# Another order and another queue for the first eight microseconds of a two-layer kernel

## The chip, the cores and the metric

The kernel runs on one core of a Trainium2 chip. The metric is the device time of one execution in microseconds (us). Before the change it is 358.14 us, the median of three runs (357.95 to 358.57).

The core's engines are named as the profile names them: PE is TensorE (matmul), PEld its loads of weights (the stationary operand, 128 columns), DVE is VectorE, ACT is ScalarE, POOL is GpSimd and SP is SyncE. SP and ACT both issue DMAs; each has a queue of its own. In a profile line, `f_0gu<-xt,w` means that tile f_0gu is written from xt and w.

## The reference

The input x has the shape 4 x 512 x 256 (batch, positions, features). There are two layers of the form

```
xn = layernorm(x)
s  = mixer(xn)                    # layer 0: a linear recurrence of one step; layer 1: causal attention
h  = silu(xn @ W1.T) * (xn @ W3.T)    # 256 -> 1024
g  = silu(fwht(h) @ W2.T)             # fwht: Walsh-Hadamard transform along the 1024
x  = x + s * g
```

The change touches only the start of layer 0: the layernorm of batch 0, its transposition, and the first products with W1 and W3.

## The kernel before, in words

**Numbers.** A matrix that goes into a product is split into a high part (a cast to fp32r by ACT) and a low part (the difference, by DVE); `split` (L59) does both. A product is then three matmuls: high x high, low x high, high x low. So each operand has two producers, one after the other: ACT's cast and DVE's subtraction.

**Work.** Batches are worked off one after the other. `ffn` (L474) makes the hidden layer in eight chunks `c` of 128 features. For each chunk there are two PSUM tiles `gu` (the gate from W1 and the linear part from W3), filled by the up products. ACT applies silu to the first, DVE multiplies by the second. The up weights w13 come in four quarters of 512 columns, each for two chunks; a quarter is one DMA from HBM, ACT's cast and DVE's subtraction. `load_w13` (L114) issues the DMA; the first quarter is fetched in two halves of 256 columns, one for each of chunks 0 and 1. `split_w13` (L122) makes the parts; for the first quarter each half by itself.

**The first batch.** `load_x` (L99) fetches x in four pieces of 128 positions, by SP's queue and ACT's in turn. `norm_first` (L381) is a generator. Up to its first yield it writes the layernorm's statistics and the normalised tiles `xn`, two pairs of tiles, on DVE, with the power -0.5 on POOL. After it come the transposes on PE, whose other operand is the identity (fetched at L949), in two groups of four (one per pair of tiles), then ACT's casts into the high part of `xt` (L426) and DVE's subtractions into the low part (L429). The first pair goes into two PSUM tiles, one per half of the features, so that it takes two casts; the second goes into one and takes one. For chunk 0 the up products are done separately for the first and the second pair (`parts=2`, L518), in the order w high x x high, w low x x high, w high x x low (L526), each with two halves of the features and two PSUM tiles: twelve matmuls of 256 columns per pair.

**Fillers.** `zero_products` (L944) multiplies a tile of zeros `zr` by itself into a PSUM tile `warm` that nobody reads. `norm_first` puts eleven of them ahead of the first group of transposes and two between the groups. Each is a matmul of 512 columns.

**What sets the order.** The program is written through a layer that records instructions and schedules them; `after(ins)` (L471) holds an instruction behind another one on its engine. The order of each queue is then fixed. The main code (L934 to L971) issues in this order: the four pieces of x (SP and ACT in turn), ACT's load of the silu table with a tiny activation (L937), the memset of `zr` (L941), on SP the identity, the halves of the first quarter, the second quarter, the two halves of w2 (`load_w2`), the Hadamard matrix, quarters 2 and 3, and the mixer's weights. `prep_first` (L974) prepares w2 beside the products. SP issues its DMAs one after the other; from the ninth DMA of the program on, an issue also waits until an earlier DMA that uses the same semaphore has landed.

On ACT, as built, the order after the table is: the cast of w13's first half, the three casts of x, the cast of the second half, the cast of quarter 1, silu of chunk 0, the cast of quarter 2, silu of chunk 1, the cast of the Hadamard matrix. On DVE: the memset, statistics and normalising, low part of w13's first half, three low parts of x, low part of the second half, two operations of w2's preparation, the gate product of chunk 0, two more of w2, low part of quarter 1.

Of the kernel before, what the change touches and what calls it, by code (L numbers as in the profile page):

```python
# [21 lines left out]
P = 128  # L22
D = 256
B = 4
S = 512
# [10 lines left out]
def kernel(ctx: ExitStack, tc: tile.TileContext, a: dict, out: bass.AP):  # L36
# [16 lines left out]
    def small(name):  # L53
        return act.tile([P, NT], F32, tag="small", name=name, bufs=16)
# [4 lines left out]
    def split(src, hi, lo, engine=nc.vector):  # L59

        h = nc.scalar.copy(hi, src)  # L61
        return h, engine.tensor_tensor(lo, src, hi.bitcast(F32), ALU.subtract)  # L62
# [51 lines left out]
    def load_w13(layer, q):  # L114

        raw = t4(f"w13raw_{layer}_{q}", [P, 2, S])
        n = 2 if (layer, q) == (0, 0) else 1
        for cs in (slice(i * S // n, (i + 1) * S // n) for i in range(n)):
            nc.sync.dma_start(raw[:, :, cs], a[f"w13_{layer}"][q][:, :, cs])
        return raw  # L120

    def split_w13(layer, q, raw):  # L122
        both = wp.tile([P, 2, 2, S], F32R, tag="w13", name=f"w13_{layer}_{q}", bufs=4)
        hi, lo = both[:, 0], both[:, 1]
        if q:

            with after(first["silus"][q - 2] if q > 1 else None):
                split(raw, hi, lo)
            return hi, lo
        halves = [slice(c * D, (c + 1) * D) for c in range(2)]  # L130
        split(*(z[:, :, halves[0]] for z in (raw, hi, lo)))
        next(normed)
        with after(first["norm"][0]), after(first["norm"][1]):
            hi_, lo_ = split(*(z[:, :, halves[1]] for z in (raw, hi, lo)))
        first["w13"] = hi_, lo_
        return hi, lo

    def load_w2(layer):
# [242 lines left out]
    def norm_first():  # L381

        xn = act.tile([P, NT, D], F32, tag="xn", name="xn0_0", bufs=3)
        hi, lo = xTs[0, 0] = xt_pair("xt0_0")
        xns[0, 0] = xn
        x = xs[0]
        ins, pairs = None, []
        for i in range(2):
            st = act.tile([P, NT, 6], F32, tag="stats", name=f"ln0_0st{i}", bufs=4)
            mv = act.tile([P, NT, 2], F32, tag="mv", name=f"ln0_0mv{i}", bufs=4)  # L390
            r = small(f"ln0_0r{i}")
            with after(ins):
                for t in (2 * i, 2 * i + 1):
                    ins = nc.vector.bn_stats(st[:, t, :], x[:, t, :])
                for t in (2 * i, 2 * i + 1):
                    with after(ins):
                        nc.vector.bn_aggr(mv[:, t, :], st[:, t, :])
                rs = r[:, 2 * i : 2 * i + 2]
                ins = nc.vector.tensor_scalar(
                    rs, mv[:, 2 * i : 2 * i + 2, 1], LN_EPS, None, ALU.add  # L400
                )
            nc.gpsimd.tensor_tensor(rs, rs, mhalf[:, :2], ALU.pow)
            pairs.append((mv, r))
        for i, (mv, r) in enumerate(pairs):
            for t in (2 * i, 2 * i + 1):
                with after(ins):
                    ins = nc.vector.tensor_scalar(
                        xn[:, t, :], x[:, t, :], mv[:, t, 0:1], r[:, t : t + 1], ALU.subtract, ALU.mult
                    )
        yield  # L410

        hi_ = lo_ = None
        ins = zero_products(11)
        for i in range(2):
            ts_ = slice(2 * i * P, 2 * (i + 1) * P)

            ks = (slice(0, 2),) if i else (slice(0, 1), slice(1, 2))
            os = [psum(f"xt0_0tp{i}{j}", [P, k.stop - k.start, 2 * P]) for j, k in enumerate(ks)]
            with after(ins):
                for t in (2 * i, 2 * i + 1):  # L420
                    for o, k in zip(os, ks):
                        for n in range(k.start, k.stop):
                            ins = transpose(o[:, n - k.start, sl(t - 2 * i)], xn[:, t, sl(n)], ident)
            for o, k in zip(os, ks):
                with after(hi_):
                    hi_ = nc.scalar.copy(hi[:, k, ts_], o)  # L426
            for o, k in zip(os, ks):
                with after(lo_):
                    lo_ = nc.vector.tensor_tensor(  # L429
                        lo[:, k, ts_], o, hi[:, k, ts_].bitcast(F32), ALU.subtract  # L430
                    )
            if i == 0:
                with after(ins):
                    ins = zero_products(2)
        first["norm"] = hi_, lo_
        yield

# [33 lines left out]
    def after(ins):  # L471
        return tc.issue_after(ins.ins) if ins else nullcontext()

    def ffn(name, xT, w13, w2, slot, defer=1, spare=(), parts=1, behind=False, tail=()):  # L474

# [31 lines left out]
        for c in range(NH):  # L509
            with after(gates[-2] if behind and c >= 2 else None):  # L510
                wh, wl = w13(c // 2)
            gu = []
            for j in range(2):

                o = psum(f"{name}gu{c}_{j}", [P, S], **(DN[0] if behind and c == 1 else GU))
                cols = slice((c % 2) * D + j * P, (c % 2) * D + (j + 1) * P)
                gu.append((o, cols))
            for half in range(parts if c == 0 else 1):  # L518
                n = S // (parts if c == 0 else 1)
                ts_ = slice(half * n, (half + 1) * n)  # L520
                if parts == 1 or c:
                    for o, cols in gu:
                        last_up = mm3(o[:, ts_], k_pairs((wh, wl), cols, xT, ts_))
                    continue

                for n, (w, x) in enumerate(((wh, xT[0]), (wl, xT[0]), (wh, xT[1]))):  # L526
                    for k in range(2):
                        for o, cols in gu:
                            last_up = matmul(
                                o[:, ts_], w[:, k, cols], x[:, k, ts_],  # L530
                                start=n + k == 0, stop=n + k == 3,
                            )
            gu = [o for o, _ in gu]
            h = hid(f"{name}h{c}")
            first["silu"] = nc.scalar.activation(h, gu[0], AF.Silu)
            first.setdefault("silus", []).append(first["silu"])
            gates.append(nc.vector.tensor_tensor(h, h, gu[1], ALU.mult))  # L537
            first["gate"] = gates[-1]
            if c < len(spare):
                hh, hl = spare[c]  # L540
            else:
                hh = hid(f"{name}hh{c}", F32R)
                hl = hid(f"{name}hl{c}", F32R)
            if c < len(spare):
                nc.scalar.copy(hh, h)
                late.append((hl, h, hh))
            else:
                split(h, hh, hl)
            for _ in range(2 if c >= NH - 2 else 0):
                if late:  # L550
                    lo_, h_, hi_ = late.pop(0)
                    with after(gates[-1]):
                        nc.vector.tensor_tensor(lo_, h_, hi_.bitcast(F32), ALU.subtract)
            queue.append((c, hh, hl))
            ups = last_up if behind else None
            with after(gates[-1] if behind else None), after(ups):
                slot(2 * c)
            if len(queue) > defer:
                down(*queue.pop(0))
            with after(gates[-1] if behind else None), after(ups):  # L560
                slot(2 * c + 1)
# [371 lines left out]

    load_x(0, 1, (nc.sync, nc.scalar))  # L934

    table = small("table")
    nc.scalar.activation(table, mhalf, AF.Silu)  # L937


    zr = hid("zr", F32R)  # L940
    nc.vector.memset(zr.bitcast(F32), 0.0)  # L941
    warm = psum("warm", [P, S], tag="dn", bufs=2)

    def zero_products(n):  # L944
        for _ in range(n):
            ins = matmul(warm, zr[:, :P], zr, start=True, stop=True)
        return ins

    nc.sync.dma_start(ident, a["ident"])  # L949
    raw13 = [load_w13(0, q) for q in range(2)]  # L950
    raw2 = load_w2(0)
    nc.sync.dma_start(had_f, a["hadamard"])
    raw13 += [load_w13(0, q) for q in range(2, 4)]
# [56 lines left out]
        yield  # L1010


    dn = None
    for b in range(B):
        tasks = []
        if b == 0:
            prep = prep_first()
            next(prep)
            tasks.append((prep, 12))
        if b:  # L1020
            tasks.append((call(gate_all, f"g0_{b - 1}", dn, xns[0, b - 1], xs[b - 1]), 1))
# [26 lines left out]
            tasks.append((prep_s(3), 4))  # L1048
        bg = Beside(*tasks)
        if b == 0:  # L1050
            dn = ffn("f0_0", xTs[0, 0], w13, w2, bg.slot, NH, spare, parts=2, behind=True)
        else:
            tail = [run(atts[0].tq, j) for j in range(2)] if b + 1 == B else []
            dn = ffn(f"f0_{b}", xTs[0, b], w13, w2, bg.slot, tail=tail)
# [152 lines left out]
```

## Time and profile before

| | |
|---|---|
| three runs, us | 357.95, 358.14, 358.57 |
| span of the profiled execution | 356.7 us (its own time is not listed; the median lies 1.5 above the span) |
| busy: PE, PEld, DVE, ACT, POOL | 350.9, 327.5, 287.2, 197.8, 20.8 us |
| mean granted clock of TensorE | 0.998 |
| eleven zero products | from 1.45 to 6.31 us, four transposes follow |
| first up product | starts at 7.84 us |
| issues: x by ACT and by SP | 0.73 and 1.18 us each |
| issues: identity, w13's halves, quarter 1 | 1.65, 2.11, 2.81, 3.45 us, all by SP |
| landed: x (four pieces), identity | 3.23, 3.43, 3.84, 4.06; 5.66 us |
| landed: w13's halves, quarter 1, w2's first half | 6.85, 7.56, 9.67, 10.97 us |

The page gives each engine's busy time and the chain of work that ended last, followed back from the last instruction. The timeline gives instructions in order of time, neighbours of the same kind merged, and in brackets how long the engine was idle before and who ended it. Matmuls overlap in the records, since PE takes the next one up before the last has drained: what counts between two matmuls is the distance of their starts. A landing is the last of a DMA's sixteen increments of its semaphore, one for each DMA engine. All times are from the span's start.

### The profile page before, as it was taken

The numbers are of one execution on the slowest core, as the hardware profiler recorded it, in microseconds if no ns is written. First come the engines' busy times: TensorE is split into PE (matmuls) and PEld (weight loads), VectorE is DVE, ScalarE is ACT, GpSimd is POOL, SyncE is SP. The second block draws the span as 40 slices with busy tenths as digits, with TensorE's granted clock in tenths as the row PEclk, the third lists the DMA queues.
The fourth block names the chain that finished last, engine by engine and source line by source line (L and its number), as shares of the span: only waits on it lengthen the run. The fifth ranks groups of instructions, "written<-read, shape, count | busy, mean of one in ns | idle before, by whom it ended". The sixth has DMA issues, their size and how long they took to land.

```text
span 356.7 us, 6276 instructions
## 1 busy us (share of the span) xinstructions
PE 350.9 (98%) x2477; PEld 327.5 (92%) x2477; DVE 287.2 (81%) x598; ACT 197.8 (55%) x374; POOL 20.8 (6%) x22
## 2 busy tenths in 40 slices
PE   8999999999999999999999999999999999999995
PEld 6878998888988898888999999999999999999994
DVE  6899659998579938998887957989679897678646
ACT  3666166265463425674467655586555676556443
POOL 2000110300020210100110001100011000000000
PEclk9999999999999999999999999999999999999999
DMA  6935000301044317656257145662554635445401
GB/s 208 367 98 205 2 1 2 117 0 61 0 167 163 145 38 230 257 174 191 118 208 265 36 172 209 217 201 115 206 187 168 230 158 206 143 152 186 199 2 59
DMA packets 16284, 52.25 MB, mean 146 GB/s; under 512 B 1632, under 2 KB 7936, under 8 KB 16256
## 3 DMA queue, kind: packets, MB, share of 16 engines
q1 hardware_dynamic: 15968, 51.60, 40.8%
q8 instruction: 19, 0.31, 0.4%
q10 hardware_dynamic: 288, 0.26, 0.2%
q14 instruction: 9, 0.07, 0.1%
HBM read 42.40 MB, written 9.45 MB: 145 GB/s over the span
## 4 chain that ended last, share of the span: by engine, by line
PE 98%; DVE 1%; ACT 0%; issue 0%
PE f_0dn L70 6%; PE f_1dn L70 6%; PE f_2dn L70 6%; PE f_0gu L70 6%; PE f_1gu L70 6%; PE f_2gu L70 6%; PE f_3gu L70 6%; PE f_3dn L70 6%; PE sc L70 4%; PE pv L70 4%; PE o L70 3%; PE v L70 3%; PE tq L70 3%; PE warm L70 2%; PE w2ps L70 1%; PE pt L70 1%
## 5 line engine op out<-in xcount | busy, mean ns | idle before, releaser
L70 PE MATMUL f_3gu<-xt,w 128*128 128x512 f32 x96 | 25.0, 396 | 0.0
L70 PE MATMUL f_2gu<-xt,w 128*128 128x512 f32 x96 | 24.8, 395 | 0.0
L70 PE MATMUL f_1gu<-xt,w 128*128 128x512 f32 x96 | 24.8, 395 | 0.0
L70 PE MATMUL f_0gu<-xt,w 128*128 128x512 f32 (+1 forms) x108 | 24.3, 378 | 0.0
L70 PEld LDWEIGHTS f_0gu<-xt,w 128*128 128x128 f32 x108 | 18.4, 188 | 4.5 <-issue 0.7
L70 PEld LDWEIGHTS f_1gu<-xt,w 128*128 128x128 f32 x96 | 17.0, 188 | 3.1
L70 PEld LDWEIGHTS f_2gu<-xt,w 128*128 128x128 f32 x96 | 17.0, 188 | 3.0
L70 PEld LDWEIGHTS f_3gu<-xt,w 128*128 128x128 f32 x96 | 17.0, 188 | 2.9
L61 ACT CAST f_2hh<-f_2h 128x512 fp32r<-128x512 f32 x16 | 10.0, 623 | 15.6 <-DVE f_2h L537 12.4
L70 PE MATMUL f_3dn<-w2l,f_3hh 128*128 128x256 f32 x64 | 17.7, 281 | 0.0
L70 PE MATMUL f_3dn<-w2h,f_3hh 128*128 128x256 f32 x64 | 17.7, 281 | 0.0
L70 PE MATMUL f_1dn<-w2l,f_1hh 128*128 128x256 f32 x64 | 17.7, 281 | 0.0
L70 PE MATMUL f_2dn<-w2h,f_2hh 128*128 128x256 f32 x64 | 17.7, 282 | 0.0
L70 PE MATMUL f_1dn<-w2h,f_1hh 128*128 128x256 f32 x64 | 17.6, 280 | 0.0
L70 PE MATMUL f_2dn<-w2l,f_2hh 128*128 128x256 f32 x64 | 17.6, 280 | 0.0
L70 PE MATMUL f_3dn<-w2h,f_3hl 128*128 128x256 f32 x64 | 17.0, 281 | 0.0
L70 PE MATMUL f_1dn<-w2h,f_1hl 128*128 128x256 f32 x64 | 17.0, 281 | 0.0
L70 PE MATMUL f_2dn<-w2h,f_2hl 128*128 128x256 f32 x64 | 16.7, 281 | 0.0
L61 ACT CAST f_3hh<-f_3h 128x512 fp32r<-128x512 f32 (+1 forms) x17 | 10.0, 595 | 10.2 <-DVE f_3h L537 6.0
L61 ACT CAST f_1hh<-f_1h 128x512 fp32r<-128x512 f32 x16 | 9.9, 621 | 9.7 <-DVE f_1h L537 6.6
L62 DVE TENSOR_TENSOR f_2hl<-f_2h,f_2hh 128x512 fp32r<-128x512 f32 x16 | 10.9, 684 | 4.5 <-ACT f_2hh L61 4.5
L62 DVE TENSOR_TENSOR f_3hl<-f_3h,f_3hh 128x512 fp32r<-128x512 f32 (+1 forms) x17 | 11.1, 655 | 3.7 <-ACT f_3hh L61 3.6
(487 smaller groups left out, 1147.7 us busy)
## 6 DMA issues: line engine op xcount, KB each, us to landing
sw<-s SPq DMA_DIRECT2D x32, 896.0 KB, 5.9
s<-sp SPq DMA_DIRECT2D x8, 512.0 KB, 4.2
s<-sp SPq DMA_DIRECT2D x8, 384.0 KB, 2.8
w2raw<-in_w SPq DMA_DIRECT2D x4, 512.0 KB, 5.5
sraw<-in_w SPq DMA_DIRECT2D x4, 512.0 KB, 3.5
mrb<-there SPq DMA_DIRECT2D x4, 512.0 KB, 3.8
w13raw<-in_w SPq DMA_DIRECT2D x3, 512.0 KB, 7.2
x<-in_x SPq DMA_DIRECT2D x3, 512.0 KB, 3.4
```

The costliest lines, as they stand in the source:

```text
L61: h = nc.scalar.copy(hi, src)
L62: return h, engine.tensor_tensor(lo, src, hi.bitcast(F32), ALU.subtract)
L70: ins = call(*args, **kwargs)
```

## The change

Four things are changed, all in the first microseconds.

1. The first half of w13's first quarter is issued by ACT's queue, behind ACT's two pieces of x and ahead of the load of the silu table. The second half stays on SP's queue, now directly behind the identity.
2. The tile of zeros has 128 columns instead of 512, and its memset too. The products read the 128 columns four times over, so that each is still 512 columns wide.
3. Between the first group of transposes and what follows stands one zero product instead of two.
4. The second group of transposes, with its casts, stands behind the first four up products (w high x x high, for the first pair of tiles) instead of ahead of all of them. A function `between` is called in `ffn` for it, and DVE's and ACT's work for w13's second half is written out after it.

As built, each engine's order differs in these places only: on PE the sequence after the first four transposes is one zero product, four up products, four transposes, and then as before; on ACT there is the new DMA issue, and the silu of chunk 1 and the cast of the Hadamard matrix stand ahead of the cast of quarter 2 instead of behind it; on DVE only the memset's width; on SP one DMA less; POOL is the same.

```diff
--- before.py
+++ after.py
@@ -114,9 +114,11 @@
     def load_w13(layer, q):
 
         raw = t4(f"w13raw_{layer}_{q}", [P, 2, S])
-        n = 2 if (layer, q) == (0, 0) else 1
-        for cs in (slice(i * S // n, (i + 1) * S // n) for i in range(n)):
-            nc.sync.dma_start(raw[:, :, cs], a[f"w13_{layer}"][q][:, :, cs])
+        queues = (nc.scalar, nc.sync) if (layer, q) == (0, 0) else (nc.sync,)
+        n = S // len(queues)
+        for i, queue in enumerate(queues):
+            cs = slice(i * n, (i + 1) * n)
+            queue.dma_start(raw[:, :, cs], a[f"w13_{layer}"][q][:, :, cs])
         return raw
 
     def split_w13(layer, q, raw):
@@ -130,9 +132,13 @@
         halves = [slice(c * D, (c + 1) * D) for c in range(2)]
         split(*(z[:, :, halves[0]] for z in (raw, hi, lo)))
         next(normed)
-        with after(first["norm"][0]), after(first["norm"][1]):
-            hi_, lo_ = split(*(z[:, :, halves[1]] for z in (raw, hi, lo)))
-        first["w13"] = hi_, lo_
+
+        def rest():
+            next(normed)
+            with after(first["norm"][0]), after(first["norm"][1]):
+                first["w13"] = split(*(z[:, :, halves[1]] for z in (raw, hi, lo)))
+
+        first["rest"] = rest
         return hi, lo
 
     def load_w2(layer):
@@ -431,7 +437,9 @@
                     )
             if i == 0:
                 with after(ins):
-                    ins = zero_products(2)
+                    zero_products(1)
+                yield
+                ins = first["up"]
         first["norm"] = hi_, lo_
         yield
 
@@ -471,7 +479,7 @@
     def after(ins):
         return tc.issue_after(ins.ins) if ins else nullcontext()
 
-    def ffn(name, xT, w13, w2, slot, defer=1, spare=(), parts=1, behind=False, tail=()):
+    def ffn(name, xT, w13, w2, slot, defer=1, spare=(), parts=1, behind=False, between=None, tail=()):
 
 
 
@@ -524,6 +532,9 @@
                     continue
 
                 for n, (w, x) in enumerate(((wh, xT[0]), (wl, xT[0]), (wh, xT[1]))):
+                    if half == 0 and n == 1:
+                        first["up"] = last_up
+                        between()
                     for k in range(2):
                         for o, cols in gu:
                             last_up = matmul(
@@ -933,21 +944,21 @@
 
     load_x(0, 1, (nc.sync, nc.scalar))
 
+    zr = hid("zr", F32R)[:, :P]
+    nc.vector.memset(zr.bitcast(F32), 0.0)
+    warm = psum("warm", [P, S], tag="dn", bufs=2)
+
+    def zero_products(n):
+        zrs = zr.unsqueeze(1).to_broadcast([P, S // P, P])
+        for _ in range(n):
+            ins = matmul(warm, zr, zrs, start=True, stop=True)
+        return ins
+
+    nc.sync.dma_start(ident, a["ident"])
+    raw13 = [load_w13(0, 0)]
     table = small("table")
     nc.scalar.activation(table, mhalf, AF.Silu)
-
-
-    zr = hid("zr", F32R)
-    nc.vector.memset(zr.bitcast(F32), 0.0)
-    warm = psum("warm", [P, S], tag="dn", bufs=2)
-
-    def zero_products(n):
-        for _ in range(n):
-            ins = matmul(warm, zr[:, :P], zr, start=True, stop=True)
-        return ins
-
-    nc.sync.dma_start(ident, a["ident"])
-    raw13 = [load_w13(0, q) for q in range(2)]
+    raw13.append(load_w13(0, 1))
     raw2 = load_w2(0)
     nc.sync.dma_start(had_f, a["hadamard"])
     raw13 += [load_w13(0, q) for q in range(2, 4)]
@@ -1010,12 +1021,15 @@
         yield
 
 
+    def begin():
+        first["rest"]()
+        next(prep)
+
     dn = None
     for b in range(B):
         tasks = []
         if b == 0:
             prep = prep_first()
-            next(prep)
             tasks.append((prep, 12))
         if b:
             tasks.append((call(gate_all, f"g0_{b - 1}", dn, xns[0, b - 1], xs[b - 1]), 1))
@@ -1048,7 +1062,7 @@
             tasks.append((prep_s(3), 4))
         bg = Beside(*tasks)
         if b == 0:
-            dn = ffn("f0_0", xTs[0, 0], w13, w2, bg.slot, NH, spare, parts=2, behind=True)
+            dn = ffn("f0_0", xTs[0, 0], w13, w2, bg.slot, NH, spare, parts=2, behind=True, between=begin)
         else:
             tail = [run(atts[0].tq, j) for j in range(2)] if b + 1 == B else []
             dn = ffn(f"f0_{b}", xTs[0, b], w13, w2, bg.slot, tail=tail)
```

More of the change, by code (lines that the diff above doesn't have):

```diff
@@ L934 @@
     load_x(0, 1, (nc.sync, nc.scalar))
-    table = small("table")
-    nc.scalar.activation(table, mhalf, AF.Silu)
-    zr = hid("zr", F32R)
+    zr = hid("zr", F32R)[:, :P]
     nc.vector.memset(zr.bitcast(F32), 0.0)
@@ L944, in zero_products @@
     def zero_products(n):
+        zrs = zr.unsqueeze(1).to_broadcast([P, S // P, P])
         for _ in range(n):
-            ins = matmul(warm, zr[:, :P], zr, start=True, stop=True)
+            ins = matmul(warm, zr, zrs, start=True, stop=True)
         return ins
     nc.sync.dma_start(ident, a["ident"])
-    raw13 = [load_w13(0, q) for q in range(2)]
+    raw13 = [load_w13(0, 0)]
+    table = small("table")
+    nc.scalar.activation(table, mhalf, AF.Silu)
+    raw13.append(load_w13(0, 1))
     raw2 = load_w2(0)
```

## The prediction

> **What bounds the kernel now.** I read the page's chain of work first, then the same chain in order of time for the first 20 us, then the timeline around the first real products.
>
> ```profile
> PE 98%; DVE 1%; ACT 0%; issue 0%
> ```
>
> TensorE (PE) is the whole chain. In the chain's first pieces there is no wait, only PE work, but part of that work is filler: products of zeros into a tile that nobody reads.
>
> ```profile
> 0.91 0.50 DVE zr L941
> 1.41 0.04 issue
> 1.45 5.06 PE warm L70 x11
> 6.51 0.67 PE xt_0tp L70 x4
> 7.18 0.47 PE warm L70 x2
> 7.65 0.44 PE xt_0tp L70 x4
> 8.08 9.85 PE f_0gu L70 x54
> ```
>
> So the bound of this stage is read from what the fillers cover. The timeline from 5.8 to 8.5 us tells it (start, us, engine, line, operation; in brackets the idle time and who ended it):
>
> ```profile
> 5.41 0.73 DVE L407 TENSOR_SCALAR xn<-x,ln_0mv,ln_0r 128x256 f32<-128x256 f32 x2
> ...
> 5.89 0.22 PEld L70 LDWEIGHTS xt_0tp<-ident,xn 128*128 128x128 f32 x1
> 6.31 0.87 PE L70 MATMUL xt_0tp<-ident,xn 128*128 128x128 f32 x4
> ...
> 6.88 0.62 ACT L61 CAST w<-w13raw 128x512 fp32r<-128x512 f32 x1 [3.72 <-DMA w13raw<-in_w]
> ...
> 7.40 1.31 ACT L426 CAST xt<-xt_0tp 128x256 fp32r<-128x256 f32 x3
> 7.49 0.60 PE L70 MATMUL xt_0tp<-ident,xn 128*128 128x128 f32 x4
> ...
> 7.82 0.81 PEld L70 LDWEIGHTS f_0gu<-xt,w 128*128 128x128 f32 x6
> 7.84 0.87 PE L70 MATMUL f_0gu<-xt,w 128*128 128x256 f32 x5
> ```
>
> Two things are to be seen. The transposes have their first input (xn, first tile) at 5.81 and their weights loaded from 5.89, but start at 6.31, behind the eleventh zero product. And ScalarE (ACT) is idle 3.72 us until the first half of w13 lands at 6.85; it casts that half, and only then, at 7.40, casts the transposed x, although the transposes were done by about 7.1. The first up product loads its weights at 7.82, 0.05 after that cast ends at 7.77. Until then two zero products and the second pair's transposes fill PE. So the late landing is what the first up product waits for.
>
> I use one marker: the start of the fifth up product (the first with w's low part), at 8.44 now. By then the old order has run 13 zero products, 8 transposes and 4 up products; the new one 12, 8 and 4. The lists are equal from there on, in PE's order and DVE's, and ACT's has one change. PE has no hole after the marker, so the marker's shift is the change in time, if no input comes late.
>
> **The steps, with the clock's rise where it was.** The zero products start 0.427 us apart (5.88 to 6.31), those of the same width later 0.233: the trace's clock record begins at 6.86.
>
> (1) The zeros. The memset of 512 columns takes 0.485. For 128 columns I bound it by a quarter, 0.12, and by 0.17, the two-column operation at L399; 0.14 taken. PE starts at 1.11 instead of 1.45 (0.34 earlier). The repeated read streams the same 512 columns; every row's pitch follows the columns streamed, so I cost it at nothing.
>
> (2) The first transposes. The eleventh zero product leaves PE at 6.31 - 0.34 = 5.97; the weights load can start at 5.87 (5.81 and 0.05 to 0.07 of signal). An exposed cold load is 0.17 (first two loads of the trace, 1.45 and 1.62). So the transposes start at 6.04, not 6.31. Four at 0.213 end at 6.89; the old ones end at 7.02, since the clock rose in the middle. Of 0.27 earned, 0.13 is left.
>
> (3) One zero product instead of two, 0.23 saved: PE is free at 7.12.
>
> (4) The casts of x. The third transpose's record ends 0.34 after its start (6.47): 6.81. ACT begins 0.04 later, 6.85; one cast takes 0.37, the second starts 0.26 after the first: ends 7.22 and 7.49. This holds if ACT is free, so if w's half has landed by about 6.3 (cast 0.62, next may start 0.53 after it).
>
> (5) Four up products: weights at 7.27, products 0.11 later at 7.38 and 7.49; the third waits for the second cast, 7.49 + 0.05 + 0.11 = 7.65, and 7.77. Then the second pair's transposes from 7.88, 4 x 0.108 = 0.43: marker at 8.32. **Gain 0.12 us.** The fillers gone, PE now stands still from 7.12 to 7.27 and a little before the third product; what is late next is the transposes themselves (ACT's cast of x).
>
> If the clock rises before the transposes (as it may, with PE busy earlier), they run at 0.108 from 5.98, the second tile's from 6.30, end 6.52; casts from 6.62 and 6.88; up products 7.15, 7.26, 7.41, 7.53; transposes 7.65; marker 8.09. Gain 0.35, and no more, as xn at 5.81 starts this chain. I take 0.2, between the two.
>
> The Trainium skill ("TensorE: Matmul & The Clock Gate", Part 1) says that the clock is released after a busy window of about 3.4 us which runs freely and does not start with the kernel. By that rule an earlier first product moves the rise not at all or by a whole window: gain 0.12 or 0.35, as in the two sums above; the rise at 6.86, 5.4 us after the first product, does not contradict it.
>
> **Behind the marker.** The second half's cast of x ends at 8.53 + 0.59 = 9.12; the products that use it come eight pitches of 0.117 after the marker, 9.25, weights 0.11 sooner: nothing, or 0.03. The cast of w's second half then ends near 9.65, used at 10.2. VectorE (DVE) makes w's low part from 7.07 (end of xn) instead of 7.53, ready 7.76; needed at 8.2. The next tight place is w13 quarter 1's low part:
>
> ```profile
> 14.23 1.22 DVE L62 TENSOR_TENSOR w<-w13raw,w 128x1024 fp32r<-128x1024 f32 x1
> ```
>
> It ends at 15.44, and the weights that need it load at 15.50, just in time. Its chain begins with the gate product at 12.42, which follows PE through the silu; DVE's own earlier work allows 12.20. So 0.2 passes; more passes only if w2raw (landed 10.97) comes sooner.
>
> (6) Issues. ACT issues the half behind its two x pieces at about 1.67 instead of SP at 2.11. Such an issue takes 0.60 to 0.78 on SP, so ACT's table load starts near 2.3 and its activation ends near 3.85; ACT's next work waits for a landing, so it costs nothing. All that SP issues behind (w13's second half, quarter 1, w2raw, hadamard and the rest) goes out about 0.69 sooner. In the window 1.45 to 5.88 the DMA engines are 80% busy, 62% in the next, so there is room.
>
> (7) ACT's order: the second silu and the hadamard cast (0.59 and 0.30) now precede the cast of quarter 2. They fit nearly into ACT's hole, 12.38 to 13.78, while quarter 2 is on its way; its products come after 18: nothing.
>
> The sum: span 356.67 - 0.2 = 356.47. The profiled execution's own time is not listed; the median of the three runs is 358.14, 1.47 above the span, taken as what lies around it. Forecast **357.9**.
>
> **Rivals.** *Slower: the half lands no sooner.* It now shares the DMA engines with w13's second half, issued almost together, instead of leading it in one queue. Each landing has a straggler: 15 of 16 increments of the first half are in by 5.93, the last at 6.85; of the second, 7.56. The up products then stand before the transposes that used to fill the wait. In the sums above the marker comes 1.47 after ACT's first cast of x, and that 0.55 after the landing: landing + 2.02. Break-even is a landing at 6.41. At 6.85 the marker is 8.87, 0.43 late: 358.6; at 7.56, 1.15 late: 359.3. For it: the straggler; against it: the issue is 0.45 sooner and the DMA engines have room at 3.5 to 4.3. Chance 0.2.
>
> *The identity lands later.* It is the other operand of the transposes, landed at 5.66, with its last increments near 5.1 to 5.7 and twelve by 4.33. The old order could have borne about 6.1; the new one needs it by 5.83. The half's packets now come on the other queue beside it. A half takes 16 packets of 46 ns on each DMA engine: 0 to 0.74 later, so 5.66 to 6.40, and the marker moves by what exceeds 5.83: 357.9 up to 358.5. Break-even at 5.95. Chance 0.2.
>
> The skill ("DMA: Bandwidth & Descriptors", Queues, rings and completion order) says that a DMA engine takes turns between the two queues a packet of some 9 to 17 descriptors at a time. By that rule nearly the whole 0.74 could go ahead of the identity: 358.5.
>
> *Faster than forecast:* the clock early and stragglers kinder: 0.35 gained, 0.5 with luck between executions (the three runs spread by 0.62): 357.4 to 357.8. Chance 0.15. The forecast itself: 0.45.
>
> **Numbers.** Range 357.3 to 359.0: it takes in the early clock and most of the two late landings, and leaves out 359.3. 0.2% is 0.72 us, about what a measurement of this kernel can tell from no change. No sum reaches 0.72 faster; spread and what I do not see get 0.12. Slower by it needs a landing past 7.1, an identity past 6.7, or an unseen stall: 0.18. Within: 0.70.
>
> **What would show it.** Right: zero products from about 1.1; first transposes near 6.04; ACT's cast of w over before 6.8 and its cast of x waiting for PE; first up product at 7.2 to 7.4; marker at 8.1 to 8.35. Wrong: transposes waiting for a DMA; ACT still waiting for w13raw when the transposes are done; a hole in PE near 15.5; zero products more than 0.427 apart.

## The result, and the profile after

| | before | after |
|---|---|---|
| median of 21 runs, us | 358.27 (357.95 to 358.78) | 358.82 (358.62 to 360.85) |
| ratio | | 1.0017, 95% interval 1.0011 to 1.0023 |
| span of the profiled execution, us | 356.67 | 356.96 |
| eleven zero products from | 1.45 | 1.05 |
| first tile normalised (xn) | 5.81 | 6.06 |
| first transposes | 6.31 | 6.11 |
| first half of w13 landed | 6.85 | 6.65 |
| first up product | 7.84 | 7.62 |
| fifth up product | 8.44 | 8.59 |
| first product of chunk 1 | 10.30 | 10.55 |
| from there to the end of the span | 346.37 | 346.41 |

The forecast was 357.9, a gain of 0.2 us. The change costs 0.55 us between the medians. The first up product starts sooner, and still the stream that follows is later.

The page of the changed kernel, its chain by engine:

```profile
PE 96%; DMA 1%; DVE 1%; ACT 0%; ACTq 0%; issue 0%
```

Before, this line had no DMA. The same chain in order of time for the first 20 us (start, us, what; from the fourth piece on):

```profile
1.67 4.98 DMA w13raw<-in_w
6.65 0.02 issue
6.67 0.62 ACT w L61
7.29 0.28 ACT xt L432
7.57 0.04 issue
7.62 0.78 PE f_0gu L70 x4
8.40 0.43 PE xt_0tp L70 x4
8.83 9.37 PE f_0gu L70 x50
```

In the kernel before, the chain ran from the memset through eleven zero products. Now it comes from the DMA that ACT issues at 1.67: landing, ACT's cast of w13's half, ACT's cast of x, up products. The fillers are no longer on it. The timeline of the changed kernel shows what stands in between:

```profile
6.11 0.76 PE L70 MATMUL xt_0tp<-ident,xn 128*128 128x128 f32 x4 [0.80 <-DVE xn L413]
...
6.63 0.48 PE L70 MATMUL warm<-zr 128*128 128x512 f32 x1
...
6.67 0.62 ACT L61 CAST w<-w13raw 128x512 fp32r<-128x512 f32 x1 [2.87 <-DMA w13raw<-in_w]
7.20 0.64 ACT L432 CAST xt<-xt_0tp 128x256 fp32r<-128x256 f32 x2
...
7.62 0.78 PE L70 MATMUL f_0gu<-xt,w 128*128 128x256 f32 x4 [0.51 <-ACT xt L432]
...
8.23 0.60 PE L70 MATMUL xt_0tp<-ident,xn 128*128 128x128 f32 x4
```

The bracket at 7.62 is the one to read: PE stood still for 0.51 us, released by ACT's cast of x. The transposes that this cast needs were done by 6.87 at the latest, but ACT, which began the cast of the half only at 6.67, started the cast of x 0.53 later, at 7.20. In the kernel before, the same wait was filled by zero products and by the second pair's transposes; here these transposes come after it, at 8.23. The fifth product's record starts at 8.59, but the sixth follows 0.20 later and not the usual 0.117; counted back from the sixth, the stream starts at 8.67. That is the landing, 6.65, plus 2.02.

Behind it nothing is lost: from the first product of chunk 1 to the end the two profiles take 346.37 and 346.41 us, and there is no hole near 15.5 (quarter 1's low part now starts at 14.48 instead of 14.23, moved with the rest).

### The profile page after: what moved, and what is told of

Its sections match the earlier page's. It is cut to its first block, busy times and chain, and to the rows that moved or that the text cites. A ratio compares the mean times of both kernels' runs of the same rounds, so it can differ in the third digit from the quotient of the medians.

```text
span 357.0 us, 6274 instructions
## 1 busy us (share of the span) xinstructions
PE 350.3 (98%) x2476; PEld 326.6 (91%) x2476; DVE 286.7 (80%) x598; ACT 197.8 (55%) x374; POOL 20.8 (6%) x22
## 4 chain that ended last, share of the span: by engine, by line
PE 96%; DMA 1%; DVE 1%; ACT 0%; ACTq 0%; issue 0%
PE f_0dn L70 6%; PE f_0gu L70 6%; PE f_1dn L70 6%; PE f_2dn L70 6%; PE f_1gu L70 6%; PE f_2gu L70 6%; PE f_3gu L70 6%; PE f_3dn L70 6%; PE sc L70 4%; PE pv L70 4%; PE o L70 3%; PE v L70 3%; PE tq L70 3%; DMA w13raw<-in_w 1%; PE w2ps L70 1%; PE pt L70 1%
## 5 line engine op out<-in xcount | busy, mean ns | idle before, releaser
L61 ACT CAST f_2hh<-f_2h 128x512 fp32r<-128x512 f32 x16 | 10.0, 623 | 15.5 <-DVE f_2h L548 12.4
```

## The experiments

The expectations use letters. A: the wait for the half, which the new order pays one for one. B: x lands later, because ACT issues a third DMA behind its two pieces of x. C, formed when B fell: on ACT's queue the half shares the DMA engines with what SP issues beside it, and so lands later. D: a hole in PE can let TensorE's clock fall back.
For each run: the ratio to the kernel before on the same chip, the first half's landing (13th, 15th and 16th increment), the first product of chunk 1, and from there to the end of the span. All but the ratio are from one profiled execution.

| run | ratio, 95% interval | landing | chunk 1 | to the end |
|---|---|---|---|---|
| queue_only | 1.0003 (0.9994 to 1.0012) | 6.24, 6.38, 6.51 | 10.05 | 346.40 |
| order_only | 1.0006 (0.9998 to 1.0015) | 5.92, 6.19, 7.06 | 10.97 | 346.39 |
| zeros_only | 0.9999 (0.9990 to 1.0008) | 6.15, 6.45, 6.49 | 10.00 | 346.71 |
| order_zeros | 1.0003 (0.9994 to 1.0011) | 5.58, 5.66, 7.02 | 10.92 | 346.41 |
| queue_zeros | 1.0003 (0.9995 to 1.0012) | 5.93, 6.20, 6.73 | 10.20 | 346.42 |
| after_free | 0.9999 (0.9990 to 1.0008) | not waited for | 10.35 | 346.40 |
| before_free | 1.0001 (0.9992 to 1.0010) | not waited for | 10.60 | 346.39 |
| after_again | 1.0030 (1.0018 to 1.0041) | 6.40, 6.78, 7.16 | 12.61 | 346.39 |
| after_fill | 1.0020 (1.0011 to 1.0029) | 6.52, 6.59, 7.08 | 10.98 | 346.42 |
| mirror | 1.0054 (1.0029 to 1.0079) | 7.71, 8.01, 8.13 | 13.42 | 346.55 |
| mirror_fill | 1.0029 (1.0017 to 1.0041) | 6.45, 6.67, 6.69 | 10.60 | 346.38 |
| ident_act | 1.0003 (0.9994 to 1.0011) | 5.56, 6.16, 6.27 | 9.96 | 346.40 |
| control_after | 1.0027 (1.0018 to 1.0036) | 5.12, 5.97, 6.75 | 10.66 | 346.38 |
| after_gap | 1.0024 (1.0014 to 1.0033) | 5.79, 5.91, 6.14 | 10.06 | 347.07 |
| old_gap | 1.0015 (1.0006 to 1.0024) | 5.84, 5.89, 5.90 | 10.24 | 347.07 |
| after_gap2 | 1.0005 (0.9996 to 1.0013) | 5.89, 5.97, 6.11 | 10.06 | 346.58 |
| old_gap2 | 1.0003 (0.9994 to 1.0012) | 6.10, 6.29, 6.38 | 10.01 | 346.52 |
| before_shift | 1.0021 (1.0012 to 1.0030) | 6.15, 6.35, 6.53 | 10.21 | 347.18 |

A profile is one execution, and the last increment scatters: order_zeros' profile was its slowest execution (359.11 against a median of 358.34). So landings are compared over several profiles, and verdicts go by the ratios.

**One part at a time.** Where an edit let the scheduler move the up products or the splitting of w13's half, an order was held with `after`, as the kernel does elsewhere; so too in mirror, mirror_fill, ident_act, the free and the gap kernels below. Those lines are not shown.

queue_only is the kernel before with the change's first part alone (its hunks in `load_w13` and around the silu table).

> The kernel before with one part of the change: the first half of w13 is issued by ScalarE's queue behind x. Two theories of the loss of 0.55 us. A, the landing and the lost filler: the first up products wait for this half, which lands little sooner (6.65 instead of 6.85 us in the two profiles), and the transposes that filled the wait now stand behind the products. B, x late: the third DMA on ScalarE's queue makes x land later (first two pieces at 3.47 and 3.66 instead of 3.23 and 3.43), and everything starts 0.24 us later. A: in the old order the fifth up product starts 1.585 us after the landing (8.436 - 6.851), so with a landing at 6.65 it comes 0.2 sooner: 358.1, ratio 0.9994. B: x is late here too, ratio 1.0007, 358.5.

order_only is the changed kernel with the half back on SP's queue, and with 512 zeros (the lines for the zeros are left out here):

```diff
-        queues = (nc.scalar, nc.sync) if (layer, q) == (0, 0) else (nc.sync,)
+        queues = (nc.sync, nc.sync) if (layer, q) == (0, 0) else (nc.sync,)
```

> The kernel before with one part of the change: second pair's transposes behind four up products, one zero product instead of two between the groups; both halves of w13 on SyncE's queue, 512 zero columns. A (landing and lost filler): the fifth up product comes 2.02 us after the landing instead of 1.585, so 0.43 later at an equal landing: 358.7, ratio 1.0012. B (x late through ScalarE's third DMA): x is not late here, ratio 1.0000 or a little below, 358.2.

zeros_only is the kernel before with the change's second part alone, 128 zeros read four times over.

> The kernel before with one part of the change: 128 zero columns, read four times over, and the memset a quarter as wide; order and queues as before (the order of the transposes ahead of the up products is pinned). A and B alike: the zero products start 0.35 to 0.4 sooner and the transposes up to 0.25 sooner, but ScalarE still waits for w13's half, so the time is unchanged: ratio 1.0000 within 0.0004. If instead it is slower by more than that, the earlier start of TensorE or the repeated read costs something that neither theory has.

order_zeros is the line of order_only's diff alone: the changed kernel, the half on SP's queue.

> The changed kernel with both halves of w13 on SyncE's queue again: the new order, one zero product, 128 zero columns. A: as slow as the changed kernel, ratio 1.0010 to 1.0017, since the order alone costs 0.4 us at an equal landing. C: the loss goes with the queue, ratio 1.0000 to 1.0005.

queue_zeros has the queue and the zeros of the change, in the old order.

> The changed kernel without its order: w13's first half by ScalarE's queue and 128 zero columns, but the second pair's transposes ahead of the up products and two zero products between the groups. A: ratio 0.9990 to 1.0003, 0.4 to 0.6 us faster than the changed kernel beside it. C: a late landing delays the old order as well, though 0.4 less than the new: ratio 1.0005 to 1.0010.

None of the five can be told from the kernel before; only queue and order together can. That was not what A had forecast: it had 1.0012 for order_only, which that run's interval still takes in, and 1.0010 to 1.0017 for order_zeros, where 1.0003 is what C had. C in turn had 1.0005 to 1.0010 for queue_zeros, which came out at 1.0003. For queue_only A had 0.9994 and B 1.0007, and 1.0003 lies between them. A had reckoned with an equal landing on either queue; the medians do not bear that out, though three of order_only's eleven executions lie at 359.1 to 359.4, as a late half would have it. B falls with order_only and zeros_only: without a third DMA of ACT's, x's statistics start at 3.47 and 3.43, as with it (3.49). The 3.25 of the first profile was a kind execution; over all profiles here the start lies between 3.13 and 3.50. The price of the new order is read from ACT's cast of the half to the first product of chunk 1: 3.42 to 3.51 in the old order (before, queue_only, zeros_only, queue_zeros), 3.88 in the new (after, order_only, order_zeros). So at the same landing the new order is 0.37 to 0.46 later, wherever the landing decides. The old order has slack for a late half, the new one has none, and on SP's queue the half is, by the medians, mostly early enough even for the new one: so neither the queue nor the order costs anything measurable alone.

**The half out of the way.** after_free makes the parts of w13's first half from x instead of from the load, which stays but is not waited for; the up products of chunk 0 are then not the reference's. before_free is the same in the old order.

```diff
-        split(*(z[:, :, halves[0]] for z in (raw, hi, lo)))
+        with after(first["xn"]):
+            split(xs[0][:, 0:2, :], *(z[:, :, halves[0]] for z in (hi, lo)))
```

> The changed kernel with the wait for w13's first half taken away: its high and low parts are made from the first two pieces of x instead (256 columns each), which have landed by 3.7 us, so these weights are not W1's and W3's; the DMA of the half still runs. A: the up products then start as soon as x is transposed and cast, fifth product near 8.25 instead of 8.67: 0.4 less than the changed kernel, 358.4, ratio to before 1.0003. B: the lateness of x stays, 358.8, ratio 1.0015.

> The kernel before with the wait for w13's first half taken away: its parts are made from the first two pieces of x, so these weights are not W1's and W3's; the DMA of the half still runs. A: in the old order the transposes and zero products fill most of the wait, so little is gained: TensorE reaches the up products at about 7.7 to 7.9 either way, chunk 1 at 10.1 to 10.3, ratio 0.9993 to 1.0000. If the wait were worth more than the 0.4 us that the order differs by, the ratio would be under 0.9990.

With the landing gone the changed kernel's loss is gone: 0.9999. That is A, shown: what the change costs is the wait for the half. But nothing is gained in either order, so the forecast's 0.2 us was not there to be had.

**The changed kernel again, with the hole filled, and with the halves' queues exchanged.** after_again is the changed kernel as it is.

> The changed kernel once more, beside three kernels that lack one of its parts each. Theory A (the first up products wait for w13's first half; in the new order the transposes no longer fill that wait): ratio 1.0010 to 1.0017; in the profile, first product of chunk 1 at 3.88 us after the start of ScalarE's cast of the half, as in the two profiles of the new order so far (10.55 - 6.67, 10.97 - 7.09), against 3.42 to 3.51 in the three of the old order. Theory C (the half on ScalarE's queue lands late because it alternates with what SyncE's queue carries, and only in the new order does that matter): the same time, and a landing after 6.9.

after_fill, mirror and mirror_fill differ from it by the first edit, the second, and both:

```diff
-                    zero_products(1)
+                    zero_products(3)
...
-        queues = (nc.scalar, nc.sync) if (layer, q) == (0, 0) else (nc.sync,)
+        queues = (nc.sync, nc.scalar) if (layer, q) == (0, 0) else (nc.sync,)
```

> The changed kernel with three zero products instead of one between the first pair's transposes and the first up product, which fills about 0.47 us (2 x 0.233) of the hole of 0.51 us in PE there. Theory C (the loss is the late landing of w13's first half, which the new order pays one for one): the fifth up product's weights still load at landing + 2.0 or later, the ratio stays at 1.0010 to 1.0030. Theory D (the hole in PE lets the clock fall back for a window in part of the executions, and this makes most of the loss): the clock's records show no fall after its rise, the ratio is 0.9995 to 1.0008, and no run is above 360.0.

> The changed kernel with the queues of w13's two halves exchanged: the first half by SP's queue, the second by ScalarE's, so that the half that is waited for is issued last. Theory C (the two halves and the identity share the DMA engines behind x, and whichever half is issued later lands later): the first half's last increments land no sooner than 6.8, the hole in PE is 0.7 us or more, ratio 1.0020 to 1.0060. Rival (ScalarE's queue as such is the slow one): the 15th increment of the first half is at about 6.0 as in the kernels with both halves on SP's queue, ratio at most 1.0008.

> The exchanged queues with three zero products instead of one. Theory C: as with one zero product, within 0.1% of it, since the landing is the limit (the hole shrinks from 0.7 us or more by 0.47 us). Theory D: the clock stays full after its rise, no run above 360.0, and the ratio lies 0.1% or more under that of the exchange with one zero product.

after_again's profile holds something that is in no profile of the old order: a clock that rises, falls, and rises again. Its table by stretch, cut at the clock's changes (stretch: us, busy of PE, PEld, DVE, ACT, POOL with counts; granted clock, DMA share, GB/s):

```profile
4.97:8.38 3.41, 1.79 (x10) 1.02 (x8) 2.46 (x9) 1.16 (x3) 1.14 (x2) 1.00 0.94 335
8.38:11.79 3.41, 3.41 (x18) 3.41 (x18) 1.90 (x5) 1.70 (x3) 0.00 (x0) 0.50 1.03 410
11.79:15.20 3.41, 3.41 (x22) 3.00 (x22) 1.89 (x4) 0.95 (x2) 0.00 (x0) 1.00 1.05 370
```

PE was busy for 1.79 of the 3.41 us after the rise: 0.74 us went to the identity, which landed at 6.25, and 0.88 to the half. In the next stretch the clock is 0.50, and chunk 1 starts at 12.61 instead of near 10.6: 2 us. mirror's profile has the same, cut at its own changes:

```profile
6.92:10.33 3.41, 1.62 (x12) 1.32 (x12) 1.72 (x5) 1.17 (x3) 0.00 (x0) 1.00 0.96 356
10.33:13.75 3.42, 3.42 (x17) 3.42 (x17) 2.49 (x4) 2.06 (x3) 0.00 (x0) 0.50 1.03 402
```

In the profiles of after and control_after the first stretch at full clock held 2.10 and 2.31 us of PE's work, in order_zeros 1.99, and the clock stayed. So the border lies between 1.79 and 1.99 of 3.41 here. The length of a single standstill does not order the profiles in this way: order_zeros had one of 1.13 us (7.99) and kept its clock, after_again none over 0.88 and lost it. Three of mirror's eight executions show a mean clock of 0.993 to 0.995 and 361.7 to 362.1 us, the other five 0.999 or 1.0 and 359.1 to 359.8; of the changed kernel one of 21, one of 8 and none of 11 are such (360.85 and 360.81). With three zero products instead of one, none of 11 and none of 6. D is thus real, and shown for mirror's tail; it is not the changed kernel's main cost, since after_fill, with the hole mostly filled, keeps 1.0020. mirror_fill was expected by C within 0.1% of mirror, by D 0.1% or more under it, and is 0.25% under it. All of that is D's share: mirror's five executions at 359.1 to 359.8 have a mean of 359.32, the six of mirror_fill 359.33.

mirror speaks on the queues. The waited-for half is on SP's queue there, at the same place as in order_zeros; only the second half now goes by ACT's queue ahead of it. It costs 1.0029 with the hole filled, against 1.0003 for order_zeros. So ACT's queue as such is not what is slow: what counts is that another transfer is issued into the other queue at the same time. The landing of 6.8 or later that was expected of mirror came there (8.13), but not in mirror_fill's profile (6.69), which is that kernel's fastest execution (358.80).

**The identity by ACT's queue**, in the old order, so that SP issues both halves one place sooner:

```diff
+    nc.scalar.dma_start(ident, a["ident"])
     table = small("table")
...
-    nc.sync.dma_start(ident, a["ident"])
     raw13 = [load_w13(0, q) for q in range(2)]
```

> The kernel before, with the identity issued by ScalarE's queue behind x instead of by SP's, so that both halves of w13's first quarter are issued one place (0.7 us) sooner on SP's queue; zero products and the old order of transposes and up products stay. Theory C: the first half's 15th increment lands 0.2 to 0.5 us sooner than in the kernel before (about 5.6), but the cast of x after the transposes ends the wait instead, so the first up product starts at 7.4 to 7.6 instead of 7.84; ratio 0.9990 to 1.0000. Rival: the identity lands later than the normalised x (after 6.0) and the transposes wait for it; ratio 1.0003 or more.

The first up product started at 7.51, as expected, and chunk 1 at 9.96, the earliest of all profiles. The 15th increment of the half came at 6.16, not at the expected 5.6 or so, though the last one was early (6.27). The ratio is still 1.0003, above the expected range.

**The second half later.** after_gap is the changed kernel with a spare load between the identity and the second half on SP's queue; old_gap has the same in the old order, and control_after is the changed kernel once more.

```diff
+            if i:
+                spare = act.tile([P, 2, 16], F32, tag="gap", name="gap", bufs=1)
+                queue.dma_start(spare, a[f"w13_{layer}"][q][:, :, :16])
             queue.dma_start(raw[:, :, cs], a[f"w13_{layer}"][q][:, :, cs])
```

> The changed kernel with a spare load of 16 KB (no part of the computation) on SP's queue between the identity and w13's second half, so that the second half is issued at about 2.8 instead of 2.12 and the first half has its share of the DMA engines to itself 0.7 us longer. Theory C (the halves delay each other): the 15th increment of the first half lands 0.3 us or more sooner than the changed kernel's on the same chip (at about 6.0), the hole in PE shrinks, ratio 0.9995 to 1.0010. Rival (the place behind x in ScalarE's queue as such): the half lands where it does in the changed kernel, 6.4 to 6.8, ratio 1.0015 or more.

> The kernel before with the first half on ScalarE's queue and the same spare load of 16 KB in the first half's old place on SP's queue, so that every other load of SP's is issued when it was; order and zero products as before. Theory C: the half lands at about 6.0, but in the old order the casts of x end the wait, so nothing is gained beyond the scatter: ratio 0.9990 to 1.0005. Rival: a landing sooner is worth 0.3 us or more here too: ratio below 0.9990.

> The changed kernel again, on the chip of the two others. Both theories: ratio 1.0010 to 1.0035.

The landings went C's way (6.14, chunk 1 at 10.06; the control 6.75 and 10.66), the ratios did not: 1.0024 and 1.0015. Both kernels take 347.07 us from chunk 1 to the end, where nearly all others had 346.38 to 346.42 (zeros_only lost 0.28 at 15.2 to 15.4, the tight place that the forecast names behind the marker; mirror 0.15, while its clock was still low). The added tile of 128 bytes a partition was the suspect, since it presumably moves the addresses of what is allocated behind it. after_gap2 and old_gap2 put the spare load into a tile that is there anyway; before_shift gives the kernel before an added tile and a memset of it, and nothing else:

```diff
-                queue.dma_start(spare, a[f"w13_{layer}"][q][:, :, :16])
+                queue.dma_start(nwb[:, :32].rearrange("p (a b) -> p a b", a=2), a[f"w13_{layer}"][q][:, :, :16])
...
+    shift = act.tile([P, 2, 16], F32, tag="gap", name="gap", bufs=1)
+    nc.vector.memset(shift, 0.0)
```

> As after_gap, but the spare 16 KB (no part of the computation) go into a tile that the kernel has anyway and loads later, so that no address changes. If the shift of addresses made the 0.65 us: from the first product of chunk 1 to the end 346.4 again, and ratio 0.9995 to 1.0012 (Theory C: the landing of the first half at about 6.0 takes the loss away). If sharing with the second half is not the cause of the late landing: ratio 1.0015 or more.

> As old_gap, with the same tile for the spare 16 KB. If the shift made old_gap's loss: 346.4 from chunk 1 to the end and ratio 0.9985 to 1.0003; if not, 1.0010 or more.

> The kernel before with one more tile of 128 bytes a partition, which is only set to zero, at the place of after_gap's. If the shift of addresses is what costs: about 347.05 from the first product of chunk 1 to the end, and ratio 1.0013 to 1.0023. If not: 346.4 and 0.9995 to 1.0005.

before_shift is 1.0021: the tile costs 0.75 us by itself. Without it, after_gap2 is 1.0005, where the changed kernel, not measured beside it, had 1.0017, 1.0030 and 1.0027. From chunk 1 to the end after_gap2 and old_gap2 still take 346.58 and 346.52, not the expected 346.4; where these 0.1 to 0.2 us come from is open. The timeline of after_gap2:

```profile
6.01 0.76 PE L70 MATMUL xt_0tp<-ident,xn 128*128 128x128 f32 x4
6.13 0.62 ACT L61 CAST w<-w13raw 128x512 fp32r<-128x512 f32 x1 [2.33 <-DMA w13raw<-in_w]
...
6.53 0.48 PE L70 MATMUL warm<-zr 128*128 128x512 f32 x1
...
6.70 0.65 ACT L436 CAST xt<-xt_0tp 128x256 fp32r<-128x256 f32 x2
...
7.12 0.58 PEld L70 LDWEIGHTS f_0gu<-xt,w 128*128 128x128 f32 x4 [0.43 <-ACT xt L436]
7.13 0.78 PE L70 MATMUL f_0gu<-xt,w 128*128 128x256 f32 x4
```

The half's cast began at 6.13 and no longer holds the cast of x back by more than a little (6.70, where the forecast had 6.85). The DMA queues from 4.3 to 5.8 us show why (packets, MB, share of the 16 engines; q10 is ACT's queue, q1 SP's). The changed kernel:

```profile
q1 hardware_dynamic: 240, 0.28, 58.9%
q10 hardware_dynamic: 166, 0.16, 31.3%
```

after_gap2:

```profile
q1 hardware_dynamic: 457, 0.19, 48.3%
q10 hardware_dynamic: 204, 0.19, 41.0%
```

In the first, SP's queue moves 0.28 MB beside the half's 0.16; in the second the half gets as much as SP. The last packet of ACT's queue ends at 6.27 in after (6.75, 6.35 and 6.66 in after_again, control_after and after_fill) and at 5.69 in after_gap2 (5.78, 5.52 and 5.98 in after_gap, old_gap and old_gap2). Between 4.3 us and that moment SP's queue moved 419 to 491 KB in the first four, 84 to 148 KB in the last four. Of the first figures, the second half's packets of 1 KB make 198 to 251 KB and quarter 1's of 4 KB 168 to 244 KB; in the last four kernels no packet of quarter 1 had started by then. That is C, shown: the two queues take from each other what a single queue would have given to the half first. What after_gap2 does not separate is the two loads, since the spare load puts back both (their issues are at 2.81 and 3.57, against 2.12 and 2.81 in after). In mirror the second half is all that ACT's queue holds behind x, so there one such load is enough. That the two queues share is what the Trainium skill ("DMA: Bandwidth & Descriptors", Queues, rings and completion order) leads one to expect, by which a DMA engine takes turns between the queues that have work for it.

## Why the prediction was wrong, point by point

The steps that held. (1) PE started at 1.05 (forecast 1.11), and the zero products are 0.427 apart, so the repeated read costs nothing. (3) One zero product is saved; it started at 6.63 and not at the reckoned 6.89, since the clock had risen at 4.25, so by its pitch of 0.233 PE was free at 6.86 (7.12). (6) ACT issued the half at 1.67. (7) and "Behind the marker": nothing lost behind (346.41 against 346.37). The fall-back sum of the first rival held to the digit: landing + 2.02 = 8.67.

**The step that failed is (6), and with it the condition of (4).** It costed the issue of SP's loads 0.69 sooner at nothing, "so there is room". That room was taken by others: from 5.88 to 6.90, where the DMA engines had been 62% busy, they were 94% busy in after. The second half, now issued 0.45 behind the first on the other queue, and quarter 1 behind it took DMA time from the first half, and the condition of (4), "if w's half has landed by about 6.3", was not met (6.65; 7.16, 7.08 and 6.75 in after_again, after_fill and control_after). after_gap2 meets it (6.11) by one small load that puts SP's loads behind it back, and its 1.0005 cannot be told from no change. This was the first rival's mechanism, with its formula and its break-even of 6.41; it should have been the likeliest case, not one of 0.2. Worked back from the medians (1.79 around the span, 346.40 behind chunk 1, 3.90 from landing to chunk 1), the landing is, as an estimate, 6.7 to 7.15 in the changed kernel and at most 6.25 to 6.4 with the half on SP's queue; there the wait is short and the ratio 1.0003.

**Steps (3) to (5) had no gain to give.** The 0.12 (0.35 with an early clock) was reckoned against the kernel before with its half at 6.85. Where the half is no bound, the old order reaches chunk 1 at xn + 4.01 (queue_only, zeros_only, old_gap2; ident_act 4.03) and the new at xn + 4.10 (after_gap2); with the clock rising late, at 6.76 in both, at xn + 4.30 (old_gap) and 4.31 (after_free). The orders are level in the second pair, and the new one is 0.09 behind in the first. An early clock is worth about 0.3 to the old order as well (4.30 against 4.01), so the 0.35 was no gain of the change. The zero product saved (0.233) comes back while PE waits for the cast of x: in after_gap2 the first up product starts 0.60 after the zero product ahead of it (6.53 and 7.13), 0.37 more than a zero product's pitch; step (5) had 0.26 there (7.12 to 7.38). The clock did rise early in after, at 4.25, and it brought nothing, since the landing decided.

**Two sizes.** (2): the first transpose's record starts 0.05 after xn and not 0.23, though the four are then 0.16 apart where the sum for an early clock had 0.108. But xn came at 6.06 and not 5.81: the profile of before was a kind execution for x, and an unkind one for the half. The sum: what lies around the span is 1.79 us (1.78 to 1.82 in the 19 profiled executions whose time is listed), not 1.47; so the profile of before was, as an estimate, an execution of 358.46 (356.67 + 1.79), not one of the median 358.14. With 1.79 the sum would have given 358.26 and not 357.9.

**The second rival** came in part: the identity landed at 6.25 in after_again, 6.08 in after_fill and 5.83 in control_after, and the transposes waited for it there (6.39, 6.21 and 5.96). In after it landed at 5.15.

Of what would show it wrong, "ACT still waiting for w13raw when the transposes are done" was not needed to the letter: ACT got the half 0.2 before the transposes' end, and the cast's 0.62 did the rest.

**No version beats the kernel before.** after_free and before_free, with the half out of the way, lie at 0.9999 and 1.0001, ident_act, with the half issued sooner, at 1.0003. By the steady distance from xn to chunk 1, what bounds these microseconds then is x: landing, statistics, normalising, transposing, casting. No run brought x sooner, so that is argued and not shown.

## What to carry to other kernels

Before taking away filler work or reordering what stands in front of a late input, read what the filler covers, and over several executions: a landing's last increment scatters by a microsecond, and an order without slack pays all of it. In this kernel a load did not come sooner by a second queue while the loads behind it moved up as well; holding those back helped, and so did leaving both in one queue, where the first goes first. And an experiment that adds a tile needs a control that adds only the tile.

## What the runs showed of the hardware that was not expected

- The clock fell back to 0.50 for one stretch of 3.41 us after a stretch at full clock in which PE was busy for 1.79 us or less of 3.41 (after_again, mirror); with 1.99 and more it stayed. The longest single standstills in the two were 0.88 and 1.78 us; order_zeros had one of 1.13 us and no fall. The Trainium skill ("TensorE: Matmul & The Clock Gate", Part 1, on oscillation) gives as a rule of thumb that gaps over about 3.4 us are to be avoided; here much shorter ones cost 2 us. How busy PE must be was not tried in finer steps.
- The clock's first rise came between 4.25 and 7.53 us in the 20 profiles, 3.2 to 6.1 us after the first product (after, before_free), and the profiles are too few to tie it to an edit.
- The last of a load's 16 increments came up to 1.54 us after the fifteenth (the identity in after_fill: 4.54 and 6.08; the half in order_zeros: 5.66 and 7.02).
- One more tile of 128 bytes a partition, which the computation does not use, made the kernel 0.75 us slower (1.0021, 1.0012 to 1.0030). The mean of chunk products of batch 1 (f_1gu on the page) goes from 395 ns to 396 (before_shift) and 397 (after_gap); the loss is spread in small steps over the whole execution. That the shifted addresses do it is the likely reading, not shown: no address is in the traces. Which addresses matter, and whether another shift would gain, is open.
